# A dilated attention and a binary convolution on one core: the queues' order is fixed from the tenth chunk on instead of from the first

## The chip, the cores and the metric

The kernel runs on one core of a Trainium2 chip. A core has five instruction queues that run side by side: PE (the matrix engine, with PEld for its weight loads), DVE (vector), ACT (scalar and activations), POOL (GpSimd) and SP, which here only issues DMAs. Each queue runs its instructions in the order in which the program holds them; an instruction whose inputs are not there holds up all that stand behind it on its queue. The metric is the device time of one execution in microseconds (us), as the median of several runs.

## The reference: what is computed

The input x is 16 images of 56 x 56 pixels with 384 channels, in float32. Two layers follow each other, each added to its input:

```
x = x + L0(groupnorm(x))      # attention over 9 neighbours
x = x + L1(groupnorm(x))      # 3x3 depthwise convolution
```

The group norm has 32 groups of 12 channels and takes mean and variance over a whole image. L0 multiplies by w_qkv (384 to 3 x 384), splits the channels into three groups with dilations 1, 2 and 3, and in each of the four heads of a group (32 channels each) forms nine scores of a pixel's q with the k of its 3 x 3 dilated neighbours (zeros beyond the edge), a softmax over the nine, and the sum of the nine v with these weights. The result is multiplied by w_proj (384 to 384), and a bias is added. L1 is a depthwise 3 x 3 convolution whose weights are cut to their signs.

## The kernel before

**Tiling.** An image is cut into 7 chunks of 8 rows, 448 pixels; there are N = 112 chunks. Inside, the channels lie on the 128 partitions, three blocks of 128 that are also the three dilation groups, and the pixels along the free dimension. A 128 x 1344 operand is one block's 448 pixels for three neighbours.

**Three plans for a chunk.** `plan_a` loads the chunk (line 471, tile xin or xin_z), transposes it on PE (476, pt_x), copies it out on ACT (489, xa; for the first image straight into x_first, which occupies buffers of other tiles), takes statistics on DVE (491, stats) and stores it, channels first, to a DRAM scratch xd (494; 496 for the first image). `plan_b` is the attention. It loads xn from xd (520), normalises it on ACT (524), and forms on PE a k group, a v group (528, pkv) and q (528, pq) for each dilation, three accumulating matmuls each. ACT copies k and v into padded tiles (541); SP copies the rows that a chunk shares with its neighbours between two such tiles (549 the upper ones, 550 the lower). DVE multiplies q by three neighbours' k at a time (593, t): nine such products. PE sums them over the heads into ps in three bursts of 8, 8 and 11 (574); a burst can begin when the last product that it takes is there. Then the softmax: ACT copies the scores (613), PE transposes them (617, pt_s), DVE takes maximum, difference, sum, reciprocal and product (622 to 632), ACT the exponential (625) and a cast (635), POOL splits the weights into three bf16 terms (638 to 643), and SP transposes them with a DMA (646, aT). In the next chunk's time PE spreads the weights over the channels (660, pb_a, nine times; one buffer in PSUM), DVE multiplies them by v (671, w), POOL adds them up (681 to 685, y). PE projects (699, po), DVE adds bias and residual (703, xr, loaded at 689), takes statistics (707), and SP stores x1d (710). `plan_c` is the convolution of a chunk; it starts ten chunks after the chunk's attention and plays no part in the first nine. The sums that turn an image's statistics into means and scales are in `group_norm` (pm, pb, pv, pp; 352 to 399).

**Once, at the start.** Weights are loaded and transposed; `load_taps` (257) brings the convolution's taps with nine small loads on SP, and `small_weights` (275 to 322) turns them and the bias into what the kernel needs: bias (277), spread (290), the signs (296 to 301), kcol (307 to 309), kdiag (318).

**Buffers.** ps_mt has three buffers for pkv, pt_x, po, pt_s and others; pq, ps and pb_a have one each; z_p (xin_z) two, xin one, xn three, xa two, xr one, t and w four each.

**What sets the order.** Every piece of a plan has a due time, from the table WHEN: a chunk's attention begins at 9 times its number (STEP = 9), its parts at offsets from there. The pieces are traced in the order of their due times, and to what is traced between the due times FROM and UNTIL a rule is applied that keeps each queue in this order:

```
        for ins in reversed(new):
            ...
            prev = newest.get(ins.engine)
            newest[ins.engine] = ins
            if prev is not None and ins.engine in engines:
                tc.add_manual_dep(
                    ins, prev.name,
                    ...
                    reason="stage order",
                )
```

For what is traced outside these times the scheduler of the programming layer decides: it takes, engine by engine, the instruction of the highest priority (the earliest traced) that is ready by its own account of durations, and only keeps the dependences of the data. For such pieces `in_one_go`, which issues the matmuls of a burst, marks them to stay together. Pieces with negative due times (the weights, the first image's transposes, the first k groups) are outside already.

Of the kernel before, what the change touches and what calls it, by code (L numbers as in the profile page):

```python
# [69 lines left out]
def dilated_attention_then_binary_conv(  # L70
# [33 lines left out]
    N = B * NCH  # L104
# [319 lines left out]
    def at(when, piece):  # L424

        pieces.setdefault(round(when, 4), []).append(piece)
# [523 lines left out]
    STEP = 9  # L950
    FIRST = -200
    FIXED = [getattr(mybir.EngineType, name) for name in FIXED_ENGINES]
    FROM, UNTIL = 0, STEP * N + 14
    at(FIRST + .14, load_weights)
    for cc in range(NG):
        at(FIRST + 6 + 2 * cc + .12, lambda cc=cc: turn_qkv_weights(cc))
# [84 lines left out]
```

## Time and profile before

| | |
|---|---|
| median of 3 runs | 5095.06 us (5094.93 to 5096.68) |
| the profiled execution | 5091.71 us |
| its span, first to last instruction | 5089.7 us |
| busy: PE / DVE / ACT / POOL | 4883.7 / 4434.3 / 2476.1 / 4253.3 us |
| mean granted clock of PE | 0.977 |
| the page's chain that ended last | PE 78%, DVE 6%, POOL 5% of the span |

By stretches of the span, PE is busy 29.9 us of the first 60, 406.7 of the 448 up to 508 us, 4158.9 of the 4192 up to 4700 us, and 288.3 of the last 389.7. The first nine chunks lie between about 60 and 460 us.

How the lines are read: a line of the instructions in order of time has start, duration, queue, source line, operation, output and inputs, the partitions and elements of both, how many of them follow each other (xN), and in brackets how long the engine had been idle before, and what released it. A float32 matmul counts as two passes, so a group of three matmuls is x6, the burst of 8 is x16 and that of 11 is x22. The granted clock is the share of full speed that PE's clock had.

### The profile page before, as it was taken

How to read it: one execution, taken by the hardware profiler on the slowest of the kernel's cores; microseconds unless marked ns; L12 is line 12 of the kernel's file. 1: busy time of each engine (PE TensorE's matmuls, PEld its weight loads, DVE VectorE, ACT ScalarE, POOL GpSimd, SP SyncE). 2: the span in 40 equal slices, each digit the busy share in tenths (PEclk: the TensorE clock that was granted, in tenths of full speed). 3: DMA queues.
4: the chain of work that ended last, by engine and by line, in shares of the span. 5: the costliest groups of instructions: out<-in, count | busy, mean ns of one | idle time of the engine just before them, and what ended most of it. 6: DMA issues, size and time to landing. Idle time of an engine off the chain costs nothing.

```text
span 5089.7 us, 72426 instructions
## 1 busy us (share of the span) xinstructions
PE 4883.7 (96%) x25093; PEld 2242.3 (44%) x25093; DVE 4434.3 (87%) x4575; ACT 2476.1 (49%) x4365; POOL 4253.3 (84%) x2998
## 2 busy tenths in 40 slices
PE   6899999999999999999999999999999999999975
PEld 4344444444444444444444444444444444444422
DVE  3788998989989998998989899898998999888866
ACT  3122555545555455555555555454555545455445
POOL 2566888888888988988888898888888888899981
PEclk8999999999999999999999999999999999999976
DMA  5334666666666666666666566666666666555555
GB/s 161 110 111 117 171 174 173 175 174 177 175 173 170 166 176 173 177 174 172 175 167 179 160 182 173 171 176 172 176 175 173 172 167 175 152 151 148 137 131 165
DMA packets 813955, 836.43 MB, mean 164 GB/s; under 512 B 362643, under 2 KB 782870, under 8 KB 813590
## 3 DMA queue, kind: packets, MB, share of 16 engines
q1 hardware_dynamic: 805606, 819.81, 60.1%
q10 hardware_dynamic: 7984, 12.00, 0.7%
q8 instruction: 199, 3.26, 0.3%
q14 instruction: 166, 1.36, 0.1%
HBM read 477.43 MB, written 231.21 MB: 139 GB/s over the span
## 4 chain that ended last, share of the span: by engine, by line
PE 78%; DVE 6%; POOL 5%; issue 2%; ACT 2%; DMA 2%; SPq 0%; ACTq 0%; DVEq 0%; POOLq 0%
PE pkv L528 24%; PE po L699 13%; PE pq L528 13%; PE ps L574 10%; PE pc L818 6%; PE pb_a L660 5%; PE pt_o L909 3%; PE pt_x L476 3%; DVE w L671 3%; POOL w L681 2%; DVE t L593 2%; PE pt_s L617 1%; ACT z L786 1%; POOL m L892 1%; DMA z<-x1d 1%
## 5 line engine op out<-in xcount | busy, mean ns | idle before, releaser
L681 POOL TENSOR_TENSOR w<-w 128x1344 f32<-128x1344 f32 x672 | 2052.2, 3054 | 448.4 <-DVE w L671 438.4
L671 DVE TENSOR_TENSOR w<-pb_a,v 128x1344 f32<-128x1344 f32 x1008 | 1562.7, 1550 | 347.0 <-PE pb_a L660 302.5
L593 DVE TENSOR_TENSOR t<-pq,k 128x1344 f32<-128x1344 f32 x1008 | 1512.8, 1545 | 56.5 <-PE pq L528 46.3
L528 PE MATMUL pkv<-xn,wqkvT 128*128 128x448 f32 x3924 | 1553.8, 541 | 0.0
L528 PEld LDWEIGHTS pkv<-xn,wqkvT 128*128 128x128 f32 x3924 | 727.8, 190 | 648.0 <-issue 617.6
L699 PE MATMUL po<-y,wprojT 128*128 128x448 f32 x2016 | 824.6, 546 | 18.6 <-POOL y L685 18.0
L528 PE MATMUL pq<-xn,wqkvT 128*128 128x448 f32 x1962 | 811.4, 550 | 0.0
L574 PE MATMUL ps<-t,sel 128*32 128x448 f32 x6048 | 664.7, 549 | 36.6 <-DVE t L593 36.4
L892 POOL TENSOR_TENSOR m<-m 128x1344 f32<-128x1344 f32 x210 | 639.0, 3043 | 10.8 <-ACT m L882 1.5
L786 ACT ACTIVATE z<-z,mrz 96x448 f32<-96x448 f32 x840 | 570.2, 751 | 101.8 <-DVE mrz L414 97.1
L882 ACT ACTIVATE m<-zg,ktap 128x448 f32<-128x448 f32 x945 | 540.4, 655 | 9.8 <-ACT zg L860 0.4
L541 ACT COPY v<-pkv 128x448 f32<-128x448 f32 x336 | 179.0, 533 | 742.2 <-DVE w L671 380.7
L699 PEld LDWEIGHTS po<-y,wprojT 128*128 128x128 f32 x2016 | 369.2, 192 | 320.0 <-issue 283.2
L528 PEld LDWEIGHTS pq<-xn,wqkvT 128*128 128x128 f32 x1962 | 350.3, 192 | 253.8 <-issue 253.5
L541 ACT COPY k<-pkv 128x448 f32<-128x448 f32 x336 | 180.1, 536 | 547.2 <-PE pkv L528 547.2
L685 POOL TENSOR_TENSOR y<-y,w 128x448 f32<-128x448 f32 x336 | 381.8, 1136 | 26.3
L684 POOL TENSOR_TENSOR y<-w 128x448 f32<-128x448 f32 x336 | 381.3, 1135 | 26.2
L660 PE MATMUL pb_a<-aT,spread 24*128 24x448 bf16 x3024 | 369.5, 360 | 20.6 <-DVE w L671 18.6
L660 PEld LDWEIGHTS <-spread 24*128 24x128 bf16 x3024 | 100.3, 91 | 636.8 <-issue 627.5
L489 ACT COPY xa<-pt_x 128x448 f32<-128x448 f32 x315 | 167.8, 534 | 433.7 <-PE pt_x L476 406.0
L818 PE MATMUL pc<-z,kdiag 96*32 96x440 f32 x3360 | 358.0, 544 | 16.5 <-POOL z L789 15.5
L574 PEld LDWEIGHTS ps<-t,sel 128*32 128x32 f32 x6048 | 190.4, 110 | 390.6 <-issue 293.4
(141 smaller groups left out, 4649.7 us busy)
## 6 DMA issues: line engine op xcount, KB each, us to landing
z<-x1d SPq DMA_DIRECT2D x570, 224.0 KB, 5.2
xr<-xd SPq DMA_DIRECT2D x112, 672.0 KB, 4.5
x1d<-xr SPq DMA_DIRECT2D x112, 672.0 KB, 5.4
xn<-xd SPq DMA_DIRECT2D x109, 672.0 KB, 4.9
xin<-in_x_dram SPq DMA_DIRECT2D x105, 672.0 KB, 8.2
xd<-xa SPq DMA_DIRECT2D x315, 224.0 KB, 2.6
out_dram<-osb SPq DMA_DIRECT2D x420, 168.0 KB, 2.4
x<-x1d SPq DMA_DIRECT2D x80, 560.0 KB, 4.2
```

The source lines that it names most:

```text
L528: nc.tensor.matmul(dst[:, :PX], wqkvT[:, cc, o0 : o0 + P], had["xn"][:, cc, :], start=(cc == 0), stop=(cc == NG - 1))
L574: return nc.tensor.matmul(had["ps"][32 * j : 32 * j + 32, :PX], sel[:, s0 : s0 + 32], tk, start=(issued[j] == 1), stop=(issued[j] == len(r ...
L593: nc.vector.tensor_tensor(t.rearrange("p k (r w) -> p k r w", w=W), q3, k3, ALU.mult)
L660: return nc.tensor.matmul(pb[:, kx, :PX].rearrange("p (s n) -> p s n", s=NSUB), spread[rows_of, v % 2, :], had["a"][rows_of, :, v // 8, :] ...
L671: nc.vector.tensor_tensor(w.rearrange("p k (r w) -> p k r w", w=W), pb[:, :, :PX].rearrange("p k (r w) -> p k r w", w=W), three(kv[1][g][m ...
L681: nc.gpsimd.tensor_tensor(w0, w0, w, ALU.add)
L685: nc.gpsimd.tensor_tensor(y, y, w0[:, 2], ALU.add)
L699: nc.tensor.matmul(po[:, :PX], wprojT[:, g, j * P : (j + 1) * P], had[f"y{g}"], start=(g == 0), stop=(g == NG - 1))
L786: nc.scalar.activation(z, z, AF.Identity, bias=mrz[:, j, q, 0:1], scale=mrz[:, j, q, 1:2])
L818: return nc.tensor.matmul(pcr[q * HD : (q + 1) * HD, :, x0:x1], kdiag[:, kx // 2, j * NQ + q, :], rows(set_of(j, q))[:, :, x0 + kx - 1 : x ...
L882: nc.scalar.activation(rows(t[:, kx]), zp[:, ky : ky + ROWS, kx : kx + W], AF.Copy, scale=ktap[:, JG, o : o + 1])
L892: nc.gpsimd.tensor_tensor(had["m"], had["m"], t, ALU.add)
```

## The change

One number: FROM goes from 0 to 9 x STEP = 81.

```
     STEP = 9
     FIRST = -200
     FIXED = [getattr(mybir.EngineType, name) for name in FIXED_ENGINES]
-    FROM, UNTIL = 0, STEP * N + 14
+    FROM, UNTIL = 9 * STEP, STEP * N + 14
     at(FIRST + .14, load_weights)
```

Pieces with due times from 0 to 80 are no longer held in the traced order; the scheduler places them. These are the pieces of chunks 0 to 8, the tenth chunk's early ones, and `small_weights` (due 5.14). From due time 81 on the order is fixed as before.

More of the change, by code (lines that the diff above doesn't have):

```diff
@@ L952, in dilated_attention_then_binary_conv @@
     FIXED = [getattr(mybir.EngineType, name) for name in FIXED_ENGINES]
-    FROM, UNTIL = 0, STEP * N + 14
+    FROM, UNTIL = 9 * STEP, STEP * N + 14
     at(FIRST + .14, load_weights)
```

## The prediction

> **What bounds the kernel now.** I read the page's busy row and slices first, then busy time by stretch, then the waits and the instructions in order of time inside the stretch that the change touches.
>
> ```profile
> PE 4883.7 (96%) x25093; PEld 2242.3 (44%) x25093; DVE 4434.3 (87%) x4575; ACT 2476.1 (49%) x4365; POOL 4253.3 (84%) x2998
> ...
> PEclk8999999999999999999999999999999999999976
> ```
> ```profile
> 60.00:508.00 448.00, 406.66 (x1810) 184.19 (x1808) 343.78 (x352) 94.93 (x174) 243.55 (x175) 0.96 0.40 112
> 508.00:4700.00 4192.00, 4158.86 (x21624) 1904.01 (x21622) 3796.87 (x3857) 2170.75 (x3827) 3726.02 (x2489) 1.00 0.64 171
> ```
> Columns: stretch, its length, busy time of PE, PEld, DVE, ACT, POOL, then granted PE clock. From 508 us on PE is busy 99% at full clock; the later order is not changed, so that part keeps its length and moves as a block. In 60 to 508 us, the first nine chunks plus the tenth's start, PE idles 41.3 us and its clock is 0.96. Only there, and in the 60 us of preparation, can time go or come.
>
> The long idle times of PE there, in order of time:
> ```profile
> 81.60 2.09 PE L574 MATMUL ps<-t,sel 128*32 128x448 f32 x16 [3.43 <-DVE t L593]
> ...
> 106.36 4.29 PE L574 MATMUL ps<-t,sel 128*32 128x448 f32 x22 [5.71 <-DVE t L593]
> ...
> 145.90 4.70 PE L574 MATMUL ps<-t,sel 128*32 128x448 f32 x22 [5.42 <-DVE t L593]
> ...
> 193.07 4.70 PE L574 MATMUL ps<-t,sel 128*32 128x448 f32 x22 [3.10 <-DVE t L593]
> ...
> 237.14 2.46 PE L574 MATMUL ps<-t,sel 128*32 128x448 f32 x22
> ...
> 338.61 3.09 PE L574 MATMUL ps<-t,sel 128*32 128x448 f32 x16 [1.91 <-DVE t L593]
> ...
> 380.37 1.71 PE L574 MATMUL ps<-t,sel 128*32 128x448 f32 x16 [1.92 <-DVE t L593]
> ```
> Each is PE standing at a score burst for a product t of DVE, and most bursts after a gap also run slow (22 passes 4.70 us against 2.46). DVE is late because its fixed order makes it stand for something else first:
> ```profile
> 79.33 0.75 DVE L318 TENSOR_TENSOR kdiag<-small 96x256 f32<-96x256 f32 x2
> 80.00 1.54 DVE L593 TENSOR_TENSOR t<-pq,k 128x1344 f32<-128x1344 f32 x1
> ...
> 98.21 1.15 DVE L491 BATCH_NORM_STATS2 stats<-xa 128x6 f32<-128x448 f32 x2 [2.03 <-ACT xa L489]
> 101.30 0.63 DVE L491 BATCH_NORM_STATS2 stats<-xa 128x6 f32<-128x448 f32 x1 [1.94 <-ACT xa L489]
> 101.84 4.47 DVE L593 TENSOR_TENSOR t<-pq,k 128x1344 f32<-128x1344 f32 x3
> ```
> The three t at 101.84 could have begun at 97.2, when their pq was done; four statistics that wait for transposes stand ahead of them.
>
> **The change, part by part.** No instruction is added or removed. Pieces due at 0 to 80 (chunks 0 to 8) lose the "stage order" edges; the program's scheduler orders them. The built orders differ from about 20 us on every engine (SP's and POOL's too), up to PE's burst that stands at 420.51 now; from there they are equal. Durations from before: three-matmul group (pq, pkv, po) 2.27, burst of 8 products 1.64, of 11 2.39, weight broadcast pb_a 0.29, transposes pt_x 0.44, DVE t or w 1.46, ACT copy 0.53.
>
> (1) Small weights. L290 to L318 leave the slot between the second and third t (76.35 to 80.00, 3.65 us) and go among the first bn_stats. There L296 waits for the tap loads, whose last three issue up to 34.96 and land a median 4.1 us after issue: about 37 to 39. Then 3.4 us of small work and seven bn_stats of 0.53 end near 45.6; the first normalisation starts about 1.3 us later (0 if they land at 36; 7 if the last takes the slowest landing of its kind, 12.7).
>
> (2) SP. The first residual load and two input loads move ahead of the eighth input. At 672 KB and some 300 GB/s that is 4.6 us more queue; with two stores it lands near 54.8, and PE wants it at 55.2 plus 1.3. I take 0, bounds 0 and 3. The first halo copies come ahead of three stores: now t waits 3.9 us for "DMA k<-k", later it does not.
>
> (3) Chunks 0 to 2. I walked the new orders with these durations: each instruction starts when its engine has done the one before it and its inputs are there.
> Chunk 0. PE does twelve transposes, three k groups, twelve more, two k groups and pq; pq ends at 73.7 (now 73.2). DVE: two t from 73.8 to 76.8, the bias copy, the third t to 78.4. PE has a v group, a k group and four transposes until 78.7, so the burst starts at 78.9 instead of 81.60. The second set of t (83.7 to 88.1) is done before PE comes to its burst (88.6). The third pq ends at 92.7; one t goes ahead of two statistics, the last ends at 98.3; PE has transposes, two k groups for chunk 2 until 98.6: no gap, and the 11-burst ends at 101.0. Now the same work (burst and k group) ends at 112.9: gain 11.9.
> Chunk 1. pq and pt_s of chunk 0, then v and k groups, transposes, two bursts without a gap (110.8, 119.1). Between them the first pb_a: the softmax's last product ends at 110.3, the cast at 111.0, POOL takes 3.1, the transposing DMA lands 4.0 after issue: 118.3; PE is there at 117.8, stall 0.5. Before the 11-burst one wait is new: an xn buffer comes free only with the last pq of chunk 1 (123.1), its load takes 5, its activation stands on ACT ahead of a transpose copy, and that copy's statistics ahead of the last t, which ends at 131.6; PE has stood 2.0 by then. pt_s ends at 135.9; now 154.2, with one matmul (0.75) less done: gain 19.
> Chunk 2. One pb_a stands 0.9 behind a late w; bursts at 147.0, 156.7, 168.1; pt_s ends at 173.9, now 201.7: gain 27.8.
>
> (4) Chunks 3 to 8. The new order puts pt_x and one matmul of a pkv ahead of the first burst:
> ```
> before: pq  pkv pkv  pb_a            burst8  pb_a  pt_x  pq  pkv pkv    pb_a        burst8
> after:  pq  pkv pkv  pb_a  pt_x pkv/3 burst8  pb_a        pq  pkv2/3 pkv pb_a  pt_x  burst8
> ```
> 0.44 + 0.75 = 1.2 us of the 1.9 us gap are filled; the rest, 0.7, is DVE's own path: from pt_s it has the same twelve operations up to the third t (now 286.7 to 298.4), only w and one t move ahead of pieces of the softmax. Walked round, a period is 38.5 us, now 163.8/4 = 41.0 (298.46 to 462.29). Gain 2.4 a chunk, four times 9.8, plus 1.6 for the chunk at 258, and about 1 before it.
>
> The walk sums to 40 us with every hand-over on time and PE at full clock. The other way round, from above: PE's idle times from 60 to 462 sum to 35.8, and slow bursts cost 12.5 (0.4, 1.8, 2.5, 2.7, 1.9, 1.6, 1.6, each against the same group at full clock): 48.3. What remains: 1.3, 0.5, 2.0, 0.9, 0.4; the normalisation wait (pp, 2.2 now, same POOL chain) 2.6; 0.7 five times; slow clock 1.9 behind pp and 1.5 once more: 14.6. Gain 33.7. I take the second, 33: a walk without any hand-over cost is an upper end.
>
> **The clock, row and rule.** [...] The rows differ: behind equal gaps of 1.9 us the burst took 3.09 at 338.61 (granted clock 0.55 over it) and 1.71 at 380.37 (clock 1.00). [...] By the rows they can: 33. I go by the rows; equally, a remaining gap of 0.7 may now and then cost up to 1.6, five times 8 us, which I keep for the range and take as 0.
>
> **Covers that the new order uses up.** POOL does rest (L638 to L643) behind two adds and two sums of the group before; aT is ready about 299.7 instead of 295.9 in the frame of the chunk at 298 and lands at 303.7. Its first pb_a comes at 309.0. Slack falls from 9.9 to 5.3 us: no cost, unless late. SP now has x1d's store and the next residual load side by side, one xr buffer: the load waits for the landing (5.4), SP is shut from 290 to 295.4, and aT behind it is not ready before 299.7: no cost. Were aT late, pb_a and everything behind it on PE's queue would wait, DVE's w and POOL's sums after it.
>
> **Rivals.** (B) Half the gain: the order was made for other durations than the chip's, and one engine stands where I have it moving: tap loads at 45 (minus 6), the eighth input late (3), small gaps slowing the clock (8). 33 less 17 is 16: 5079. For it: small gaps do slow bursts. Against: tap loads of 29 to 35 us landed in about 4.
> (C) No change: DVE's length sets the chunk, PE only waits elsewhere. DVE is busy 35.0 of 40.1 us in a chunk, below PE's 38.2, which speaks against it; 5092.
> (D) Slower: aT comes late for its first pb_a. It decides when aT is 5.3 + 33/8 = 9.4 us later than worked out in all eight chunks; at 12 late, 8 x 6.7 = 54 is lost against 33 won: 5116. For it: POOL's adds now stand ahead of rest, and SP is shut in between. Against: 9 us is three whole adds.
> (E) The change does nothing: excluded, the orders differ.
>
> **How the numbers follow.** The profiled execution took 5091.7 (span 5089.7); the runs' median is 3.4 higher, 5095.1. The sum is a difference, so 5095 - 33 = 5062. Chances: A 0.74, B 0.13, C 0.06, D 0.07. A's own range is 5053 to 5074 (walk's 40 plus 2 to spare; 33 less 12). For 8 in 10: 5051 to 5083, which takes B in. A difference under 0.2% (10 us) cannot be told from none. Faster 0.87, same 0.06, slower 0.07.
>
> **What would show it.** DVE's kdiag at about 40 us instead of 79; first 11-burst done near 101 and at full clock; chunk 2's pt_s near 174; bursts 38.5 us apart with gaps of 0.7 under it; PE idle in the first 480 us near 15 instead of 41; everything after shifted by one constant. Wrong if PE waits for pb_a on aT, DVE stands at L296 beyond 40, or the period stays at 41.

## The result, and the profile after

The changed kernel takes 5054.57 us (median of 6 runs, 5051.24 to 5064.65), the kernel before, run in turn with it, 5096.36 us (6 runs, 5094.93 to 5099.93). The ratio is 0.9922, with a 95% interval of 0.9909 to 0.9935: 41.8 us faster, where 33 were forecast and 5062 us. The profiled execution took 5055.87 us, its span 5053.9.

The page's busy row of the changed kernel, and its busy time by stretch (columns as before: stretch, length, busy time of PE, PEld, DVE, ACT, POOL, granted PE clock, DMA share, GB/s):

```profile
PE 4881.6 (97%) x25093; PEld 2243.3 (44%) x25093; DVE 4432.0 (88%) x4575; ACT 2479.5 (49%) x4365; POOL 4254.4 (84%) x2998
```
```profile
60.00:423.65 363.65, 356.11 (x1568) 160.82 (x1566) 301.44 (x290) 87.49 (x158) 216.24 (x143) 0.99 0.41 116
```
The same question to the kernel before, up to the same instruction:

```profile
60.00:462.29 402.29, 363.99 (x1569) 164.18 (x1568) 307.35 (x308) 86.15 (x158) 216.32 (x143) 0.96 0.38 110
```
Both stretches end at the first score burst of the tenth chunk, 462.29 before and 423.65 after, and hold 1568 or 1569 recorded matmuls. The stretch is 38.64 us shorter. The length less PE's busy column is its idle time: 38.3 before, 7.5 after, so 30.8 of the gain is idle time. The other 7.9 is the busy column itself, 363.99 less 356.11: the same matmuls ran quicker, at a clock of 0.99 instead of 0.96.

The instructions of PE in order of time, after, at the places that the prediction showed of before:

```profile
77.66 1.71 PE L574 MATMUL ps<-t,sel 128*32 128x448 f32 x16
...
96.76 2.46 PE L574 MATMUL ps<-t,sel 128*32 128x448 f32 x22
...
116.35 0.37 PE L660 MATMUL pb_a<-aT,spread 24*128 24x448 bf16 x3 [0.23 <-DMA aT<-e]
...
128.96 2.46 PE L574 MATMUL ps<-t,sel 128*32 128x448 f32 x22 [1.00 <-DVE t L593]
...
166.78 4.15 PE L574 MATMUL ps<-t,sel 128*32 128x448 f32 x22 [1.88 <-DVE t L593]
...
173.91 0.65 PE L617 MATMUL pt_s<-perm,sT 128*112 128x128 f32 x4
...
307.44 1.71 PE L574 MATMUL ps<-t,sel 128*32 128x448 f32 x16
...
345.98 1.71 PE L574 MATMUL ps<-t,sel 128*32 128x448 f32 x16
...
423.65 1.71 PE L574 MATMUL ps<-t,sel 128*32 128x448 f32 x16 [1.93 <-DVE t L593]
```
The first three long gaps (3.43, 5.71, 5.42 us) have become none, none and 1.00, and the two 11-bursts behind them run at 2.46 instead of 4.29 and 4.70. One late and slow burst is left, at 166.78; chunk 2's pt_s behind it starts at 173.91, where the forecast had it end near 174. From 307.44 to 345.98 is a period of 38.54 without a bracket; the last line is the first chunk with a fixed order again, and the gap of 1.93 is back.

DVE in order of time, after:

```profile
34.99 0.18 DVE L296 TENSOR_SCALAR small<-small 96x36 f32<-96x36 f32 x1 [4.18 <-DMA small<-in_L_conv_w_dram]
...
36.78 0.41 DVE L318 TENSOR_TENSOR kdiag<-small 96x256 f32<-96x256 f32 x1
...
53.10 0.17 DVE L399 COPY mr<-pp 128x6 f32<-128x6 f32 x1 [4.97 <-PE pp L396]
...
91.17 1.56 DVE L593 TENSOR_TENSOR t<-pq,k 128x1344 f32<-128x1344 f32 x1 [1.08 <-PE pq L528]
92.64 1.15 DVE L491 BATCH_NORM_STATS2 stats<-xa 128x6 f32<-128x448 f32 x2
93.70 3.00 DVE L593 TENSOR_TENSOR t<-pq,k 128x1344 f32<-128x1344 f32 x2
...
160.25 0.63 DVE L491 BATCH_NORM_STATS2 stats<-xa 128x6 f32<-128x448 f32 x1 [3.20 <-ACT xa L489]
160.79 1.54 DVE L593 TENSOR_TENSOR t<-pq,k 128x1344 f32<-128x1344 f32 x1
```
The small weights (kdiag) are done at 37 instead of 80. The t of the first 11-burst start at 91.17 and 93.70, with two statistics between them; before, four statistics that had to wait stood ahead of all three, and they began at 101.84. The last two lines are what remained: at 160.25 statistics again stand ahead of t, for 3.20 us, and PE's burst at 166.78 pays.

### The profile page after: what moved, and what is told of

The parts are those of the page before. It is cut to its first block, busy times and chain, and to the rows that moved or that the text cites. A ratio compares the mean times of both kernels' runs of the same rounds, so it can differ in the third digit from the quotient of the medians.

```text
span 5053.9 us, 72462 instructions
## 1 busy us (share of the span) xinstructions
PE 4881.6 (97%) x25093; PEld 2243.3 (44%) x25093; DVE 4432.0 (88%) x4575; ACT 2479.5 (49%) x4365; POOL 4254.4 (84%) x2998
## 4 chain that ended last, share of the span: by engine, by line
PE 83%; DVE 5%; POOL 5%; DMA 3%; issue 2%; ACT 2%; SPq 0%; ACTq 0%; POOLq 0%; DVEq 0%
PE pkv L528 26%; PE pq L528 14%; PE po L699 13%; PE ps L574 10%; PE pc L818 6%; PE pb_a L660 5%; PE pt_x L476 3%; PE pt_o L909 3%; DVE w L671 2%; POOL w L681 2%; DVE t L593 1%; PE pt_s L617 1%; DMA z<-x1d 1%; ACT z L786 1%; POOL y L684 0%
## 5 line engine op out<-in xcount | busy, mean ns | idle before, releaser
L892 POOL TENSOR_TENSOR m<-m 128x1344 f32<-128x1344 f32 x210 | 639.1, 3043 | 10.8 <-ACT m L882 1.5
L660 PE MATMUL pb_a<-aT,spread 24*128 24x448 bf16 x3024 | 368.5, 359 | 19.2 <-DVE w L671 17.5
```

The costliest lines, as they stand in the source:

```text
L660: return nc.tensor.matmul(pb[:, kx, :PX].rearrange("p (s n) -> p s n", s=NSUB), spread[rows_of, v % 2, :], had["a"][rows_of, :, v // 8, :] ...
L892: nc.gpsimd.tensor_tensor(had["m"], had["m"], t, ALU.add)
```

## The experiments

A "lead" below is the difference of two starts: how much earlier than in the profile of before a chunk's 11-burst begins. In the changed kernel it is 9.6 in the first chunk (106.36 to 96.76), 16.9, 26.3, and 38.65 in the tenth (486.44 to 447.79). A lead is good to about 3 us, since the start-up itself moves: with the same order in the first chunks, the kernel below that is free from the fourth to the ninth chunk has its first 11-burst at 103.61, and before at 106.36.

### Only the small weights earlier

```
-    at(5.14, small_weights)
+    at(-2.14, small_weights)
```
All else as in the kernel before, with its fixed order from the first chunk.

> Only small_weights is taken out of the fixed order (due time -2.14 instead of 5.14); all else is fixed from 0 as before. Theory (gains add up by place): DVE loses 3.65 us between its second and third t, the first burst of chunk 0 starts near 78 us instead of 81.60, and everything behind it moves by 3.5: about 5093. Rival (the stall only moves to the next burst): the first burst is early, but the 11-burst still starts at 106.4 and the time stays at 5096.

Measured: 5088.83 us against 5093.38 (ratio 0.9992, interval 0.9983 to 1.0). PE of this kernel, in order of time:

```profile
99.05 4.70 PE L574 MATMUL ps<-t,sel 128*32 128x448 f32 x22 [5.72 <-DVE t L593]
...
291.97 1.71 PE L574 MATMUL ps<-t,sel 128*32 128x448 f32 x16 [1.92 <-DVE t L593]
332.12 2.94 PE L574 MATMUL ps<-t,sel 128*32 128x448 f32 x16 [1.91 <-DVE t L593]
```
The lead is 7.3 in the first chunk and 6.5 in the tenth: the gap before the first burst is gone, and every later gap stands at its old length. Some 2 us of the lead were there before any burst (the first pq begins at 68.92 instead of 70.90). The gap of 3.43 and the slow matmuls behind it (11.10 us from the first burst to the second before, 9.47 here) make 5.1, and the medians say 4.6. So the small weights are worth some 5 us of the 42. The last two lines are of use further down: equal gaps, and bursts of 1.71 and 2.94.

### The first three chunks, and the six behind them

```
-    FROM, UNTIL = 0, STEP * N + 14
+    FROM, UNTIL = 3 * STEP, STEP * N + 14
```


> Free order for the pieces due from 0 to 26 (chunks 0 to 2), fixed from the fourth chunk on. Theory: chunks 0 to 2 carry 28 to 29 us of the gain, so about 5068; the period of chunks 3 to 8 is 41.0 as before, with gaps of 1.9. Rival (the early gain is given back where the fixed order catches up with later buffers or loads): above 5080.

```
-        newest["pinned"] = FROM <= when < UNTIL
+        newest["pinned"] = FROM <= when < UNTIL and not 3 * STEP <= when < 9 * STEP
```


> Fixed order for pieces due from 0 to 26, free from 27 to 80, fixed again from 81. Theory: chunks 3 to 8 alone carry about 11 to 12 us, period 38.5 instead of 41.0: about 5085. Rival (the shorter period needs the head start of chunks 0 to 2): the period stays near 41 and the time at 5094 or more. The gains of this kernel and of the one with free order for chunks 0 to 2 add up to that of the whole change (about 41) by the theory.

Measured: the first three free, 5069.17 us (0.9952, 0.9937 to 0.9967); the next six free, 5071.91 us (0.9958, 0.9943 to 0.9972); the changed kernel beside them 5054.14 us (0.9924, 0.9908 to 0.9941; this run's expectation was 

> The changed kernel once more, beside the others on one chip: 5051 to 5065, PE's first burst of the tenth chunk at 423.65 us again. Its runs lay 13 us apart while those of the kernel before lay within 5: if the spread comes from the end of the program, the profile has the same times up to 4650 us and other ones behind it; if it comes from the start, the burst at 423.65 is elsewhere.

).

PE with only the first three free:

```profile
169.67 4.15 PE L574 MATMUL ps<-t,sel 128*32 128x448 f32 x22 [3.10 <-DVE t L593]
...
188.84 1.71 PE L574 MATMUL ps<-t,sel 128*32 128x448 f32 x16 [1.58 <-DVE t L593]
...
274.67 1.71 PE L574 MATMUL ps<-t,sel 128*32 128x448 f32 x16 [1.91 <-DVE t L593]
314.82 1.71 PE L574 MATMUL ps<-t,sel 128*32 128x448 f32 x16 [1.91 <-DVE t L593]
```
The first line explains why the second kernel won twice what I gave it (21.5 us instead of 11 to 12), and the first less (24.2 instead of 28 to 29). I had cut the work in my head at the chunk, but the cut is at a due time, and chunk 2's 11-burst has due time 29. Its gap of 3.10 and slow run, and that of 1.58 in the next chunk, belong to the part behind 27. The periodic part is as expected: with the order fixed, 314.82 - 274.67 = 40.15 a chunk and a gap of 1.91; free, 38.54 and none. The two gains add up to 45.7 against 39.2 for both together. Of the excess in the leads (25.4 + 19.9 against 38.65), 2.8 is the start-up of the second kernel, which stands there before anything differs. The changed kernel's own profile beside them has the tenth chunk's first burst at 424.04, 0.4 from the first profile's: the scatter of its runs, which I had looked for at the start or the end of the program, comes from between; the last section shows more.

### One queue at a time

Five queues were freed. These kernels are the changed one, but keep the traced order of some queues up to due time 81:

```
+    KEPT = [e for e in FIXED if e not in (mybir.EngineType.DVE,)]
...
-            pin(FIXED if newest["pinned"] else ())
+            pin(FIXED if newest["pinned"] else KEPT if 0 <= when < FROM else ())
```
with DVE, PE, both, or SP in the place of DVE.

> Only DVE's order is freed for due times 0 to 80; PE, ACT, POOL and SP keep the fixed order. Theory (DVE stands for statistics that PE's later transposes release): with t ahead of them the big stalls of chunks 0 to 2 shrink (small weights 3.6, chunk 0 some 4.6 plus slow clock, chunks 1 and 2 3 to 5 each), but PE has no filler for the 1.9 us gaps of chunks 3 to 8, whose period stays 41: gain about 18, 5078. Rival (PE's order is what counts): gain under 5.

> Only PE's order is freed for due times 0 to 80. Theory: the gaps of chunks 3 to 8 are filled (about 11) and in chunks 0 to 2 PE's earlier transposes release DVE's statistics sooner, part of the rest: gain about 20, 5076. Rival (DVE's order is what counts): gain only the 11 or less; or a loss, if PE's new order waits for a t that DVE's old order brings late.

> PE and DVE freed together, ACT, POOL and SP fixed. Theory: these two carry nearly all: gain 36 to 41, 5055 to 5060. Rival (SP's earlier halo copies and ACT's order matter too): gain under 30.

> Only SP's order is freed. Theory: the wait of t for a halo copy (3.9 us) ended only 0.26 us after its pq, so 0 to 1 us: 5096. Rival: DMAs moved ahead delay others: 5 us or more slower.

| free up to the tenth chunk | median, us | ratio to before (interval) | lead at the tenth chunk |
|---|---|---|---|
| DVE | 5072.16 | 0.9959 (0.9945 to 0.9974) | 19.3 |
| PE | 5072.39 | 0.9962 (0.9947 to 0.9977) | 23.1 |
| PE and DVE | 5060.74 | 0.9940 (0.9925 to 0.9954) | 32.4 |
| SP | 5095.90 | 1.0005 (0.9997 to 1.0014) | -4.6 |
| all five | 5054.14 | 0.9924 (0.9908 to 0.9941) | 38.3 |

DVE alone, PE in order of time:

```profile
95.80 3.99 PE L574 MATMUL ps<-t,sel 128*32 128x448 f32 x22 [2.79 <-DVE t L593]
...
281.77 1.71 PE L574 MATMUL ps<-t,sel 128*32 128x448 f32 x16 [1.28 <-DVE t L593]
291.82 1.71 PE L574 MATMUL ps<-t,sel 128*32 128x448 f32 x16 [0.43 <-DVE t L593]
```
PE alone:

```profile
99.83 3.87 PE L574 MATMUL ps<-t,sel 128*32 128x448 f32 x22 [3.40 <-DVE t L593]
...
292.30 1.71 PE L574 MATMUL ps<-t,sel 128*32 128x448 f32 x16 [0.36 <-DVE t L593]
331.22 1.71 PE L574 MATMUL ps<-t,sel 128*32 128x448 f32 x16 [0.36 <-DVE t L593]
```
The two queues cut the same gaps from both sides. A free DVE makes t earlier: the first 11-burst's gap falls from 5.71 to 2.79, but in the steady chunks 1.28 is left and 0.43 comes new, so that the period stays at 40.2, since PE's fixed order puts nothing else there. A free PE puts transposes and part of a k or v group ahead of the burst: the steady gap falls to 0.36 and the period to 38.9, but at 99.83 it still stands 3.40, because DVE holds t behind statistics. Both together reach 32.4 of 38.3, less than the 42.4 of a plain sum; what ACT, POOL and SP add on top of them is about 6. SP alone gives nothing (its trace has even longer gaps, 7.32 and 6.50, ahead of the first two 11-bursts), so that the order of the DMA issues by itself was no hidden cost. DVE alone was 6 us and PE alone 4 us better than I expected; both together, with 33.6 us, stayed below the 36 to 41 expected.

By the traces, most of those 6 us lies with POOL's order. PE, DVE and POOL with PE and DVE free:

```profile
319.37 1.71 PE L574 MATMUL ps<-t,sel 128*32 128x448 f32 x16 [0.99 <-DVE t L593]
```
```profile
313.36 1.56 DVE L671 TENSOR_TENSOR w<-pb_a,v 128x1344 f32<-128x1344 f32 x1 [2.62 <-POOL w L681]
```
```profile
307.13 1.16 POOL L638 TENSOR_TENSOR rest<-ew,e 112x512 f32<-112x512 f32 x1 [7.40 <-ACT e L635]
...
310.31 6.15 POOL L681 TENSOR_TENSOR w<-w 128x1344 f32<-128x1344 f32 x2
```
POOL with all five free:

```profile
336.46 6.16 POOL L681 TENSOR_TENSOR w<-w 128x1344 f32<-128x1344 f32 x2
```
In its traced order POOL stands 7.40 us for the cast e, with two adds behind it whose products w have been ready since 302.7. DVE's next w waits 2.62 for the first of these adds, t stands behind that w, and PE waits 0.99. With all five free, POOL does the two adds at 336.46, ahead of its rest at 345.01, and PE's gap is gone. From the fourth to the ninth chunk the changed kernel's lead grows by 10.7, this one's by 6.4. A kernel with POOL alone, or ACT alone, freed beside PE and DVE was not run.

### Where the free order should end

The free order won wherever PE waited. Should it go on?

```
-    FROM, UNTIL = 9 * STEP, STEP * N + 14
+    FROM, UNTIL = 12 * STEP, STEP * N + 14
```
and the same with 16 and 30.

> The order is fixed from the thirteenth chunk on (due time 108), so the tenth to the twelfth are free too. If the free order is better wherever TensorE waits, this takes away what is left there after the change: the gap of 1.93 us ahead of the tenth chunk's first burst, that of 0.37 ahead of the next and perhaps part of the 2.7 us that the pair products wait for in that chunk: 2 to 4 us below the changed kernel, about 5051. If the free order lengthens chunks in which TensorE never waits, the three chunks cost more than they give: 5055 to 5058.

> Fixed from the seventeenth chunk on. The theory that only the idle time of TensorE was to be had: the same as from the thirteenth, within 1 us, since TensorE is 99% busy there in both orders. The rival, that the free order goes wrong once the banks' products come between the bursts: at least 1 us slower for each chunk set free, so 4 us or more above from12.

> Fixed from the thirty-first chunk on, so that more than twenty chunks of 42 us in which TensorE is busy all the time are free. Theory: as from12 within 2 us. Rival: 18 chunks more at 0.3 to 1 us each, 5 to 18 us slower than from12, with gaps before TensorE's bursts in those chunks.

> The changed kernel once more, beside the three others of this batch and on their chip: 5054 within 3 us, with the tenth chunk's first burst near 423.7 us again.

| fixed from chunk | median, us (range) | ratio to before (interval) |
|---|---|---|
| tenth (the change) | 5058.08 (5052.10 to 5062.01) | 0.9928 (0.9913 to 0.9943) |
| thirteenth | 5054.60 (5048.54 to 5060.00) | 0.9918 (0.9902 to 0.9935) |
| seventeenth | 5065.75 (5063.89 to 5067.35) | 0.9944 (0.9929 to 0.9959) |
| thirty-first | 5104.63 (5095.46 to 5109.09) | 1.0018 (1.0010 to 1.0026) |

Up to the thirteenth nothing is lost, and what is won cannot be measured: the intervals overlap. Its trace shows the gaps gone that I named, but new waits in their place (1.90 for POOL's z the longest), so that less than the 2 to 4 us expected was won: from the ninth to the thirteenth chunk the lead grows by 0.8 us (37.6 to 38.4), where the changed kernel's goes from 38.6 to 38.5. (The changed kernel itself, with 5058, lay 1 us above the range that I had given it here; its tenth chunk's 11-burst came 3 us later than in the first profile.) Behind that my theory, that the order cannot matter where PE is 99% busy, is wrong. The rival holds, and more strongly than I had it: the end at the seventeenth costs 11 us against that at the thirteenth (4 or more expected), the end at the thirty-first 50 (5 to 18). But the waits do not stand ahead of the bursts, where I had put them. With the free order kept to the thirty-first chunk the lead falls from 37.7 at the ninth chunk to -13.8 at the twenty-ninth, and the kernel is slower than before. PE's waits of that kernel from 466 to 1300 us (line waited for, sum, times, longest):

```profile
PE po L699 <- POOL y L685: 29.2, 15, 6.2
```
These 29.2 are the larger part of the 45.7 us that PE is idle there. The same view with the order fixed from the thirteenth chunk has 5.6 us of idle time and no wait on y at all; its longest line is this:

```profile
PE pp L396 <- POOL pair L391: 3.1, 2, 1.6
```
The wait on y is new. Its first and longest case, kernel fixed from the thirty-first chunk, PE:

```profile
500.50 5.80 PE L699 MATMUL po<-y,wprojT 128*128 128x448 f32 x8 [6.21 <-POOL y L685]
```
DVE and then POOL of the same kernel just before it:

```profile
482.38 1.55 DVE L671 TENSOR_TENSOR w<-pb_a,v 128x1344 f32<-128x1344 f32 x1
```
```profile
483.40 2.35 POOL L897 TENSOR_TENSOR m<-m 128x448 f32<-128x448 f32 x2
485.84 1.14 POOL L900 TENSOR_TENSOR xg<-m,xg 128x448 f32<-128x448 f32 x1
486.93 6.16 POOL L892 TENSOR_TENSOR m<-m 128x1344 f32<-128x1344 f32 x2
493.05 3.03 POOL L681 TENSOR_TENSOR w<-w 128x1344 f32<-128x1344 f32 x1
496.05 1.13 POOL L897 TENSOR_TENSOR m<-m 128x448 f32<-128x448 f32 x1
497.14 1.13 POOL L684 TENSOR_TENSOR y<-w 128x448 f32<-128x448 f32 x1
498.24 1.12 POOL L897 TENSOR_TENSOR m<-m 128x448 f32<-128x448 f32 x1
499.33 1.12 POOL L685 TENSOR_TENSOR y<-y,w 128x448 f32<-128x448 f32 x1
```
POOL of the kernel fixed from the thirteenth chunk, at the same work:

```profile
484.17 3.06 POOL L681 TENSOR_TENSOR w<-w 128x1344 f32<-128x1344 f32 x1 [0.68 <-DVE w L671]
...
488.52 1.14 POOL L685 TENSOR_TENSOR y<-y,w 128x448 f32<-128x448 f32 x1
```
The product w is done at 482.38 + 1.55 = 483.9 in the first kernel. In the second, POOL stands ready for it and y's last add starts at 488.52. In the first, POOL has just begun to sum up a convolution chunk (L897, L900), goes on with the adds of the next one (L892), and then mixes that one's sums between those of y, whose last add starts at 499.33: 10.8 us later, of which PE feels 6.21, and its 8 passes behind that gap run slow (5.80 us, where 12 take 4.67 at 442.61 in the changed kernel). The eleventh chunk alone loses 9.5 us of lead so; most of the free chunks from the thirteenth on take 43.7 to 44.9 us from 11-burst to 11-burst, where the fixed order takes 42.2. In the changed kernel the two rounds of L892 lie further apart, at 502.85 and in the chunk after; with the end at the thirteenth the sums that follow the first adds have their fixed place too, at 521.39. No instruction of PE waits for m or xg in the first kernel's view of waits, so nothing on PE needed them yet, while y is wanted at once, by a projection with the next chunk's matmuls behind it on PE's queue. In the first nine chunks there is no convolution, and POOL has no such choice to make. So the free order's limit, as far as these traces show, lies not where PE stops waiting, but where POOL gets a second kind of work. That is read from the traces: a kernel that frees these chunks but keeps POOL's order, which would show it, was not run. Why the scheduler places the adds so (its priorities, or its own account of when w is ready) was not tried either. No version tried beats the changed kernel measurably.

## Why the prediction was right, and where its sums were off

The mechanism held: in the first three chunks PE's gaps came from DVE's fixed order, in the steady ones from PE's having nothing else to do, they go by reordering on both, and what follows moves as a block. The budget took 33 us, 9 less than the medians and 6 less than the trace. The result lies near the far end of the range of 5053 to 5074, not in its middle. Point by point:

**(1) Small weights.** The 1.3 us that they were to cost did not come. L296 waits 4.18 us as foreseen, but the taps were there at 34.99, not at 37 to 39, and the first scale mr is at 53.10, before at 53.56. I had counted the landing of the last tap load from the end of its issue (34.96), but the 4.1 us run from its start: that issue starts at 32.56 before, and the load lands at 36.7; in the changed kernel it starts at 30.64 and lands at 34.9. The first burst starts at 77.66, 1.2 us before the forecast.

**(2) SP.** Right: taken as 0; from 40 us up to the tenth chunk PE waits for no input in the changed kernel, and SP alone free is 1.0005, with no gain or loss that can be measured.

**(3) The walk of chunks 0 to 2.** Nearly right. Gains by the ends of the 11-bursts (start plus duration, before less after): 11.4, 19.2 and 26.8, forecast by the same chunks' work 11.9, 19 and 27.8. The order of events, the new wait in front of chunk 1's 11-burst (2.0 forecast, 1.00 measured) and pb_a's wait on aT (0.5, 0.23) came as walked. Missed: the 1.88 at 166.78, with 4.15 - 2.46 = 1.7 of slow clock behind it (0.59 over the burst). I had checked for that burst whether PE had other work until then, and not whether statistics would again stand ahead of its t. It is back in all profiles of the changed kernel (2.26 and 2.03 in the others).

**(4) Chunks 3 to 8.** The period is 38.5, as forecast. Its make-up is not: I left 0.7 us to DVE's path before each burst, and none is to be seen. PE is busy 181.7 of 183.65 us from 240 to 423.65, and the rest is the gap of 1.93 at the end, so it is PE's own work that sets 38.5. Without its gap a chunk before took 40.15 - 1.92 = 38.23; in the new order, which splits pkv groups, PE's work is 0.3 longer.

**The two sums.** The walk said 40 and the trace says 38.65. The budget said 33.7, and I took it, "a walk without any hand-over cost is an upper end". The term that was mis-sized is "what remains: 14.6", in its idle part. It had 11.2 of idle time. The trace has 7.5, and 1.93 of that is the gap ahead of the tenth chunk's first burst, which both kernels have and which stood in neither side of my sum; so 5.6 remained (0.23, 1.00, 0.24, 1.88, 0.68 and 1.53). The five times 0.7 and the 0.9 never came, nor the 1.3; the 2.0 and the 2.6 (pp) were each 1.0 too large; against that the 1.88 and the 0.68 had not been foreseen. The slow clock that remained, 3.4, was right: 1.7 in the burst at 166.78, and 1.8 in the two groups behind pp (3.57 and 5.36 us at 220.14 and 223.50, at a clock of 0.80). The busy column fell by 7.9 where 12.5 - 3.4 = 9.1 was to be won; the 0.3 a chunk of (4) is of that size. In all 5.6 of idle time too much was kept back, 0.6 of small gaps was not on the list, and 1.2 of slow clock was overrated: 5.0, from 33.7 to 38.65. From there to the 41.8 of the medians is within what the runs scatter, told below; the two other batches have 39.2 and 36.6.

**The clock.** The 3.2 us that two bursts behind gaps of 1.9 had cost, those at 338.61 and 420.51, I took as time to be won (33 with them, 30 without): 11.14 and 11.15 us from each to the next burst, where the one at 298.46, behind the same gap, has 9.55. Rightly for the sum: 7.9 us of the gain are matmuls that run quicker, and the bursts that stood behind gaps of 1.9 are among them (all bursts of 8 between 183 and 424 us take 1.71 in the changed kernel). But the forecast's "most bursts after a gap also run slow" does not hold: of the fourteen that wait for t between 60 and 470 us before, six do. They are those behind 5.71, 5.42, 3.43 and 3.10 (granted clock 0.56, 0.50, 0.78 and 0.50 over the burst) and two of the five behind 1.9; one behind 2.08 is not. Two of the lines, before:

```profile
165.27 1.71 PE L574 MATMUL ps<-t,sel 128*32 128x448 f32 x16 [2.08 <-DVE t L593]
...
420.51 3.08 PE L574 MATMUL ps<-t,sel 128*32 128x448 f32 x16 [1.91 <-DVE t L593]
```
At 1.9 the gap's length alone says little: small_early's two bursts behind 1.92 and 1.91 took 1.71 and 2.94. What else decides was not shown, so the forecast's 1.6 for a gap of 0.7 remains an estimate, from the bursts behind 1.9. (The clock over the burst at 338.61, 0.55 in the forecast, reads 0.53 over the row's own stretch.)

**The rivals.** B (half the gain) falls: its three costs were tap loads at 45 (35 measured), the eighth input (PE waits for no input) and five slowed bursts (none after 240 us). C (DVE sets the chunk) falls by the period of 38.5. D (aT late) falls: pb_a waits on aT once, for 0.23. But a loss of its kind, a wait on what POOL delivers late because its adds stand in another order, is the one that makes the kernel slower than before when the free order goes on to the thirtieth chunk.

## What to carry to other kernels

An order written out by hand is tuned for the steady state; check it apart for the start, where some of the pipeline's stages do not run yet and other work could fill the gaps. When such an order is loosened, look at the queue that serves two consumers of different urgency: there a scheduler's free choice can cost more than all the gaps it closes elsewhere (some 2 us a chunk here), even with the engine that sets the time 99% busy. In a forecast, take the idle time of both kernels as length less busy time between the same two instructions, and treat every remaining wait as something to be traced, not as a margin.

## What had not been expected of the hardware

The runs of one kernel scatter by 13 us (5051.24 to 5064.65), and the traces show where part of it comes from. At the changes of image, seven chunks apart, PE waits about 1.6 us for the pair sums (pp; 1.53 to 1.60 in the changed kernel, but 2.67 at 459.09), and what follows runs at full clock or not: the q group behind pp takes 2.52 us there, or between 3.47 and 4.22. The changed kernel, PE in order of time:

```profile
1062.63 0.83 PE L396 MATMUL pp<-pair,gselT 32*128 32x4 f32 x6 [1.59 <-POOL pair L391]
1063.38 3.72 PE L528 MATMUL pq<-xn,wqkvT 128*128 128x448 f32 x6
1067.04 1.02 PE L408 MATMUL pz<-pair,gselT 32*32 32x2 f32 x48
1067.99 6.45 PE L528 MATMUL pkv<-xn,wqkvT 128*128 128x448 f32 x12
```
and the kernel before, at the same place in the program and in the same fixed order:

```profile
1101.15 0.83 PE L396 MATMUL pp<-pair,gselT 32*128 32x4 f32 x6 [1.58 <-POOL pair L391]
1101.91 2.52 PE L528 MATMUL pq<-xn,wqkvT 128*128 128x448 f32 x6
1104.36 0.68 PE L408 MATMUL pz<-pair,gselT 32*32 32x2 f32 x48
1104.96 4.78 PE L528 MATMUL pkv<-xn,wqkvT 128*128 128x448 f32 x12
```
The same gap to 0.01 us, and 11.2 us for the three groups against 8.0, of which 2.4 remain in the chunk's length; the granted clock over the 20 us around them is 0.83 and 1.00. The chunk with the change of image takes 46.38 us between its 11-burst and the one before in the kernel before (1089.86 to 1136.24), 48.82 here (1051.33 to 1100.15), and 47.68 in another execution of the changed kernel (1051.71 to 1099.39). Each such place draws about 0, 1.3 to 2.0 or 2.4 us (twice, in other kernels of this document, 4.1), and there are some fifteen of them. Over the twelve between the eighteenth and the ninety-fifth chunk these draws sum to 14.5, 8.0 and 13.2 us in three profiles of the changed kernel, and to 8.7 in that of the kernel before. This is also why the profiled execution's span is only 35.8 us shorter, and not 38.65: its lead falls to 34.2 at the chunk that begins near 4718, by such places in the two kernels. What decides the draw was not settled.
